# A GpSimd drain inside the last layer, one load of sums for four heads, and another order of the first loads

## The chip, the cores and the metric

The kernel runs on 1 core of one Trainium2 chip. The core has five engines with a queue of instructions each: TensorE (PE; its weight loads are listed as PEld), VectorE (DVE), ScalarE (ACT), GpSimd (POOL) and SyncE (SP). SP, ACT and POOL issue DMAs, which all run on the core's 16 DMA engines. The metric is device time in microseconds (us) of one execution, the median of several runs.

## The reference

Four graph layers run one after another on a matrix `x` of 4096 nodes by 256 features, with one random 0/1 adjacency of 4096 x 4096 (density 0.0078). Behind each layer stands `x = layernorm(x + layer(x))`. Cut to what matters here:

```python
# layer 0: attention over ALL pairs; pairs without an edge count with logit 0
node_feats = (x @ W.T + b).reshape(N, 8, 32)
logits = leaky_relu(parent[:, None, :] + child[None, :, :], 0.2)
logits = where(adj != 0, logits, 0.0)
out = einsum('ijh,jhc->ihc', softmax(logits, axis=1), node_feats)
# layer 1: (diagonal(adj) + adj) @ (x @ weight) + bias
# layer 2: two steps of a top-p attention (0.9) and of a diffusion, then layer norm
# layer 3: relu(concat([x, adj @ x / max(deg, 1)]) @ W + b)
```

## The kernel before

**Layer 0** is done in two passes. `sums0` walks over all row blocks with float32 matmuls (L601). Per row and head it makes the part of the softmax sums that belongs to the pairs without an edge above a threshold, and stores it in DRAM as `zd` (block, row, head, 33 values: 32 features and the sum of weights). It also stores the factors `gmd` in bfloat16, the adjacency as bytes in `nad`, and the parents' logits in `lpd`.

The second pass, the *heads* (578 to 1288 us), loops over `half` (2 halves of four heads), `it` (4 tiles of 1024 rows) and `hh` (4 heads): 32 heads in time. For each head and each of 8 groups of 4 neighbour blocks a mask `gt` is made. A comparison of the parents' logits `lpb` with the children's `nlc` gives `sg`, on ACT (L276, five groups of eight) or on DVE (L270, three), and DVE ANDs it with the adjacency bytes `na` (L278, L272). PE multiplies the mask with the factors `gm` (L331, 32 matmuls for a group, 256 for a head). Then DVE sums up the head: L337 (reduce), L341, L344, L345 (adds `z`, the tile loaded from `zd`), L347 and L348 (divide, into `y`).

The loads of this pass: `na` (L301) and `gm` (L303, L306) on SP; `lpb` (`row_logits`, L236) and `z` (L316) on POOL, both with two buffers, one load for each head; `X` and the first half's `y0` on SP (L308, L310). In the very first head the masks of groups 0 and 1 (`gt0`), their factors (`gm0`) and the first `lpb` (`first`) are there already; this is what `begun = 2` says, and why the loop over the loads starts with group 2 there. `mask` buffers: four `gt`, three `sg`. In the second half POOL also adds up `X` (L362, L363) and does layer norms (L88, L89, L96).

`add_w1` loads the weights of layer 1 and of the attention of layer 2: `load_w` and `load_row` on ACT (L115, L121), the rest on POOL (L783, L784). It stands in the code at the last tile of the second half, but the heads are not in a `manual_schedule`: the framework orders each engine's instructions there, and these loads depend on nothing that comes late, so the profile shows them issued at 579 to 600 us.

**Layer 3** (`layer3`, from 3723 us) is not in a `manual_schedule` either. For each row block `b` from 6 to 31 PE does 32 matmuls (L1973). `ready(b + 2)` has the pieces of the adjacency cast from bytes two blocks ahead, half on DVE (L1940) and half on ACT (L1942), into 8 buffers. `close(b, ps)` loads `x` (L1979, queued on ACT), scales on ACT (L1981), adds on DVE (L1982 to L1986), normalises (L85 and L86 on DVE, `ln_var` L88 and `ln_rstd` L89 on POOL, `y` L96 on DVE) and stores on ACT's queue (L1989). The first six passes of the loop also close one of the blocks 0 to 5, whose products layer 2 made. POOL issues no DMA in this layer.

At the end of the tile context (L2051) the framework itself puts a drain and a meeting of all engines.

Of the kernel before, what the change touches and what calls it, by code (L numbers as in the profile page):

```python
# [9 lines left out]
F32 = mybir.dt.float32  # L10
# [13 lines left out]
P = 128  # L24
# [26 lines left out]
def row_broadcast(v, n):  # L51

    return bass.AP(tensor=v.tensor, offset=v.offset, ap=[[0, P], [1, n]])


class Net:
# [159 lines left out]
    def layer0(self):  # L216
        nc, tc, NB, D, N = self.nc, self.tc, self.NB, self.D, self.N
        H, C = 8, 32
        C1 = C + 1
        IT = min(1024, N)  # L220
        Q = IT // P
        keep = self.ctx.enter_context(tc.tile_pool(name="l0k", bufs=1, space=DRAM))
        self.fits = keep.tile([1, 1], I32, name="fits")
        with ExitStack() as ctx:
            pool = ctx.enter_context(tc.tile_pool(name="l0", bufs=1))
# [6 lines left out]
            fac = pool.tile([P, 4, NB, H], F32, name="fac")  # L232
            lpd = dram.tile([H, N], F32, name="lpd")

            def row_logits(t, h, it):
                nc.gpsimd.dma_start(t, bass.AP(tensor=lpd.tensor, offset=lpd.offset + h * N + it * IT, ap=[[0, P], [1, IT]]))  # L236
                return t

            first = pool.tile([P, IT], F32, name="lpb0")
# [5 lines left out]
            zd = dram.tile([NB, P, H, C1], F32, name="zd")  # L245
# [42 lines left out]
            work = ctx.enter_context(tc.tile_pool(name="l0w", bufs=2))  # L288
# [2 lines left out]
            gm = gp.tile([P, NB, H // 2, 6 * C1], BF16, name="gm")  # L291
            na = gp.tile([P, NB, IT], U8, name="na")

            later = []
            per_head = Q // 2 // (H // 2)
            for half in range(2):
                for it in range(N // IT):
                    i0 = it * Q
                    begun = 2 if it == half == 0 else 0
                    for g in [*range(begun, NB // K), *range(begun)]:  # L300
                        nc.sync.dma_start(na[:, g * K:(g + 1) * K], nad[it, :, g * K:(g + 1) * K, :])  # L301
                        if it == 0:
                            nc.sync.dma_start(gm[:, g * K:(g + 1) * K, 0], gmd[half, :, g * K:(g + 1) * K, 0])  # L303
                    for hh in range(1, H // 2 if it == 0 else 0):
                        for g in range(0, NB // K, 2):
                            nc.sync.dma_start(gm[:, g * K:(g + 2) * K, hh], gmd[half, :, g * K:(g + 2) * K, hh])  # L306
                    if half:
                        nc.sync.dma_start(X[:, i0:i0 + Q, :], xr[:, i0:i0 + Q, :])  # L308
                        y0 = work.tile([P, Q, D // 2], F32, name="y0", bufs=1)
                        nc.sync.dma_start(y0, yd[i0:i0 + Q].rearrange("b p d -> p b d"))  # L310
                    y = work.tile([P, Q, H // 2, C], F32, name="y")
                    for hh in range(H // 2):
                        h = half * (H // 2) + hh
                        lpb = row_logits(work.tile([P, IT], F32, name="lpb"), h, it) if h or it else first
                        z = work.tile([P, Q, C1], F32, name="z")
                        nc.gpsimd.dma_start(z, zd[i0:i0 + Q, :, h].rearrange("b p c -> p b c"))  # L316
                        acc = psum.tile([P, Q, 256], F32, name="acc")
                        for g in range(NB // K):

                            head0 = g < 2 and half == it == hh == 0  # L320
                            if head0:
                                gt = gt0[:, g * K:(g + 1) * K, :]
                            else:
                                gt = work.tile([P, K, IT], FP8, name="gt", bufs=4)
                                sg = work.tile([P, K, IT], FP8, name="sg", bufs=3)
                                mask(gt, sg, na[:, g * K:(g + 1) * K, :], lpb, g, h)
                            for k in range(K):
                                jc = g * K + k
                                for q in range(Q):

                                    nc.tensor.matmul(acc[:, q, :6 * C1], gt[:, k, q * P:(q + 1) * P],  # L331
                                                     gm0[:, jc, :] if head0 else gm[:, jc, hh, :],
                                                     start=(jc == 0 and q % 2 == 0),
                                                     stop=(jc == NB - 1 and q % 2 == 1))

                        red = work.tile([P, Q, 2 * C1], F32, name="red")
                        nc.vector.tensor_reduce(red, acc[:, :, :6 * C1].rearrange("p q (s c) -> p q c s", s=3),  # L337
                                                AX.X, ALU.add)

                        red = red.rearrange("p q (s c) -> p q s c", s=2)  # L340
                        nc.vector.tensor_mul(red, red, fac[:, 0:2, i0:i0 + Q, h].rearrange("p s q -> p q s").unsqueeze(3)  # L341
                                             .to_broadcast([P, Q, 2, C1]))
                        t1 = red[:, :, 0, :]
                        nc.vector.tensor_add(t1, t1, red[:, :, 1, :])  # L344
                        nc.vector.tensor_add(t1, t1, z)  # L345
                        r = work.tile([P, Q], F32, name="r")
                        nc.vector.reciprocal(r, t1[:, :, C])  # L347
                        nc.vector.tensor_mul(y[:, :, hh, :], t1[:, :, :C], r.unsqueeze(2).to_broadcast([P, Q, C]))  # L348
                        for xs in later[:per_head]:
                            self.layernorm(work, xs, xs, nc.gpsimd, bufs=6)  # L350
                        del later[:per_head]
                    y = y.rearrange("p q h c -> p q (h c)")
                    if not half:
                        nc.gpsimd.dma_start(yd[i0:i0 + Q].rearrange("b p d -> p b d"), y)
                        continue

                    if i0 + Q == NB:
                        self.add_w1()
                    engine = nc.vector if i0 + Q == NB else nc.gpsimd
                    for q in range(0, Q, 2):  # L360
                        xs = X[:, i0 + q:i0 + q + 2, :]
                        nc.gpsimd.tensor_add(xs[:, :, :D // 2], xs[:, :, :D // 2], y0[:, q:q + 2])  # L362
                        engine.tensor_add(xs[:, :, D // 2:], xs[:, :, D // 2:], y[:, q:q + 2])  # L363
                        later.append(xs)
            self.later = later
            acc = psum.tile([P, Q, 256], F32, name="acc").rearrange("p q c -> p (q c)")
            for c in range(2):
                half = acc[:, c * 512:(c + 1) * 512]
# [408 lines left out]

    def add_w1(self):
        nc, pool = self.nc, self.pool1
        self.weight1, self.bias1 = self.load_w(pool, self.w1, "w1"), self.load_row(pool, self.b1, "bias1")  # L780
        aw1, aw3, aw2, _ = self.attention_parts()
        for t, w in ((aw1, self.aw1t), (aw3, self.aw3t)):
            nc.gpsimd.dma_start(t, w.rearrange("(c p) m -> p c m", p=P))  # L783
        nc.gpsimd.dma_start(aw2, self.aw2t)  # L784

    def attention_parts(self):

# [1157 lines left out]
    def layer3(self):  # L1945
        nc, tc, NB, D = self.nc, self.tc, self.NB, self.D
        G = 8
        with self.ctx3 as ctx:
            pool = ctx.enter_context(tc.tile_pool(name="l3", bufs=1, side="right"))
            work = ctx.enter_context(tc.tile_pool(name="l3s", bufs=2, side="right"))  # L1950
# [26 lines left out]
            def close(b, ps):  # L1977
                x = work.tile([P, 2, D], F32, name="x", bufs=3)
                nc.scalar.dma_start(x, self.xo[b])  # L1979
                low = work.tile([P, D], F32, name="low")  # L1980
                nc.scalar.mul(low, ps[:, D:], rdeg[:, b:b + 1])  # L1981
                nc.vector.tensor_add(x[:, 1], x[:, 1], bias)  # L1982
                h = work.tile([P, 1, D], F32, name="h")
                nc.vector.tensor_add(x[:, 1], x[:, 1], low)
                nc.vector.scalar_tensor_tensor(h[:, 0], ps[:, :D], rdeg[:, b:b + 1], x[:, 1], op0=ALU.mult, op1=ALU.add)  # L1985
                nc.vector.scalar_tensor_tensor(h[:, 0], h[:, 0], 0.0, x[:, 0], op0=ALU.max, op1=ALU.add)  # L1986
                y = work.tile([P, 1, D], F32, name="y")
                self.layernorm(work, y, h)
                nc.scalar.dma_start(out[:, b, :], y[:, 0])  # L1989
# [3 lines left out]
            for b in range(6, NB):  # L1993
                ps = products(b)
                if b + 2 < NB:
                    ready(b + 2)
                if rest:
                    k = rest.pop(0)
                    close(k, self.early3[k])
                close(b, ps)  # L2000


@with_exitstack
# [51 lines left out]
```

## Time and profile before

| what | value |
|---|---|
| median of 3 runs (lowest, highest) | 3931.0 us (3929.32, 3931.58) |
| the profiled execution: its time, its span | 3932.46 us, 3930.8 us |
| busy PE, PEld | 3872.5 us (99%), 3360.1 us (85%) |
| busy DVE, ACT, POOL | 2995.1, 2742.3, 1162.8 us |
| mean granted TensorE clock | 0.995 |
| layer 0's heads, 578 to 1288 us: busy PE, DVE, ACT, POOL | 702.9, 685.4, 664.1, 178.3 us |
| layer 3 and the end, 3720 to 3931 us: busy PE, DVE, ACT, POOL | 197.3, 112.9, 66.1, 26.3 us |

The span runs from the first to the last instruction of the program; the execution's own time is 1.66 us longer. A row of a timeline gives start, duration, engine, line, operation, written and read tiles, and in brackets how long the engine had been idle and who ended that. An engine name with a q (POOLq) is its sequencer: drains, semaphores and branches, which the page does not count as busy. A row of a window gives its length, then busy time (and instructions) of PE, PEld, DVE, ACT and POOL, the granted clock, the share of the DMA engines and GB/s.

### The profile page before, as it was taken

What the parts mean: (1) busy time and instruction counts of PE and PEld (TensorE: products, weight loads), DVE (VectorE), ACT (ScalarE), POOL (GpSimd) and SP (SyncE); (2) the same over time, 40 slices, a digit from 0 to 9 for tenths busy, and PEclk for the clock granted to TensorE, in tenths of its full rate; (3) what the DMA queues carried; (4) which work ended last, traced back from release to release, by engine and by line L of the source; (5) the groups of instructions that cost most, each with busy time, mean ns of one, the idle gap of its engine ahead of it and who ended that gap; (6) DMA issues with size and microseconds to landing.
All of it is one profiled execution on the core that took longest, in us unless ns stands there. A gap on an engine that the chain in (4) does not pass through costs nothing. (4 is left out here: it accounts for less than half of the span.)

```text
span 3930.8 us, 68793 instructions
## 1 busy us (share of the span) xinstructions
PE 3872.5 (99%) x25081; PEld 3360.1 (85%) x25081; DVE 2995.1 (76%) x6637; ACT 2742.3 (70%) x5121; POOL 1162.8 (30%) x1402
## 2 busy tenths in 40 slices
PE   8999999999999999999999999999999999999998
PEld 7999989999999887578888888876888888888786
DVE  6444449999999544768787878848999999999464
ACT  4443449999999322568888888836888888888232
POOL 1222220111444222411111111114566555555211
PEclk9999999999999999999999999999999999999999
DMA  4666657334221696533333232463333333336541
GB/s 119 201 206 205 219 187 214 93 108 129 73 82 60 247 384 266 151 114 109 105 101 100 95 103 93 138 220 109 109 112 114 112 115 101 107 108 205 208 149 45
DMA packets 319870, 561.58 MB, mean 143 GB/s; under 512 B 73063, under 2 KB 140151, under 8 KB 315415
## 3 DMA queue, kind: packets, MB, share of 16 engines
q1 hardware_dynamic: 244832, 401.18, 31.4%
q0 software_dynamic: 32224, 98.75, 7.8%
q10 hardware_dynamic: 42454, 57.04, 4.2%
q8 instruction: 203, 3.33, 0.3%
q14 instruction: 157, 1.28, 0.1%
HBM read 386.71 MB, written 170.13 MB: 142 GB/s over the span
## 5 line engine op out<-in xcount | busy, mean ns | idle before, releaser
L1414 PE MATMUL ps_a<-X,aT 128*128 128x256 f32 x4096 | 969.1, 379 | 1.6 <-ACT h L1558 1.1
L1414 PEld LDWEIGHTS ps_a<-X,aT 128*128 128x128 f32 x4096 | 773.2, 190 | 127.4 <-issue 3.3
L331 PE MATMUL acc<-gm,gt 128*128 128x198 bf16 x8192 | 702.9, 248 | 12.4 <-DVEq L375 5.4
L331 PEld LDWEIGHTS <-gt 128*128 128x128 fp8e4 x8192 | 700.8, 97 | 14.5 <-issue 9.7
L276 ACT ACTIVATE sg<-lpb,nlc 128x1024 fp8e4<-128x1024 f32 x632 | 664.1, 1135 | 45.4 <-DVE gt L278 32.5
L180 PE MATMUL ps_r<-XD,adj_piece 128*128 128x512 f32 x1888 | 528.4, 414 | 0.0
L601 PE MATMUL pz<-src,ar 128*128 128x264 f32 x4096 | 500.6, 285 | 0.4 <-DVE big L399 0.4
L601 PEld LDWEIGHTS pz<-src,ar 128*128 128x128 f32 x4096 | 500.4, 189 | 0.5 <-issue 0.5
L1139 ACT ACTIVATE ja<-e,nc 128x2048 uint8<-128x2048 f32 x240 | 480.9, 2004 | 2.0
L1407 ACT COPY aT<-ps_tp 128x512 f32<-128x512 f32 x512 | 295.9, 578 | 207.6 <-PE ps_tp L1405 201.6
L180 PEld LDWEIGHTS ps_r<-XD,adj_piece 128*128 128x128 f32 x1888 | 333.0, 189 | 68.8 <-issue 12.9
L1204 DVE MAX8 cand<-v 128x8 f32<-128x256 f32 x1024 | 347.1, 411 | 4.4
L1254 DVE SCALAR_TENSOR_TENSOR e<-e,edge 128x512 f32<-128x512 f32 x512 | 346.8, 749 | 2.1
L561 ACT ACTIVATE nb<-ar 128x512 uint8<-128x512 f32 x256 | 147.6, 623 | 280.0 <-DVE ar L558 164.6
L1405 PE MATMUL ps_tp<-ident,e 128*128 128x128 f32 x2048 | 307.3, 273 | 2.4 <-DVEq L1270 1.7
L1200 DVE SCALAR_TENSOR_TENSOR v<-e,hi 128x2048 f32<-128x2048 f32 x128 | 301.4, 2355 | 2.4
L1405 PEld LDWEIGHTS ps_tp<-ident,e 128*128 128x128 f32 x2048 | 255.9, 141 | 54.1 <-issue 2.6
L558 DVE CAST ar<-a 128x1024 fp32r<-128x1024 f32 x128 | 88.9, 694 | 267.3 <-PE pz L601 267.2
L270 DVE TENSOR_SCALAR sg<-lpb,nlc 128x1024 fp8e4<-128x1024 f32 x384 | 285.3, 778 | 6.7 <-SPq L375 4.6
L1048 ACT ACTIVATE e<-ps_logit 128x1024 f32<-128x1024 f32 x256 | 259.9, 1025 | 27.1 <-PE ps_logit L1046 26.8
L1046 PE MATMUL ps_logit<-kT,q 128*128 128x512 f32 x1024 | 273.9, 409 | 1.5 <-ACT e L1048 0.9
L854 PE MATMUL ps_adj<-XD,adj_piece 128*128 128x512 f32 x1024 | 239.8, 394 | 0.0
(408 smaller groups left out, 5587.4 us busy)
## 6 DMA issues: line engine op xcount, KB each, us to landing
adj_piece<-adjs SPq DMA_DIRECT2D x504, 256.0 KB, 2.8
a<-in_adjt_dram SPq DMA_DIRECT2D x256, 256.0 KB, 3.0
adjs<-adj_piece SPq DMA_DIRECT2D x96, 512.0 KB, 3.3
na<-nad SPq DMA_DIRECT2D x64, 512.0 KB, 5.4
lpb<-lpd POOLq DMA_DIRECT2D x32, 512.0 KB, 4.4
nad<-nb POOLq DMA_DIRECT2D x128, 128.0 KB, 2.7
na<-nad ACTq DMA_DIRECT2D x16, 1024.0 KB, 8.8
gmd<-gb POOLq DMA_DIRECT2D x64, 198.0 KB, 2.7
```

Source lines behind the costliest of these rows:

```text
L180: nc.tensor.matmul(ps, a[:, k, :], rhs(jc).rearrange("p s d -> p (s d)"), start=(jc == 0), stop=(jc == self.NB - 1))
L270: nc.vector.tensor_scalar(sg[:, k, :], lpb, nlc[:, 4 * g + k, h:h + 1], 2.0 ** -5, op0=ALU.is_ge, op1=ALU.mult, saturate=False)
L276: nc.scalar.activation(sg[:, k, :], lpb, AF.Sign, scale=-1.0, bias=nlc[:, 4 * g + k, h:h + 1], saturate=False)
L331: nc.tensor.matmul(acc[:, q, :6 * C1], gt[:, k, q * P:(q + 1) * P], gm0[:, jc, :] if head0 else gm[:, jc, hh, :], start=(jc == 0 and q % 2 ...
L601: nc.tensor.matmul(pz[q][:, t, :W], ar[:, q, k, :], src[:, jc, t, s], start=(jc == 0 and s == 0), stop=(jc == NB - 1 and s == 1))
L1139: nc.scalar.activation(ja, e[:, s * HALF:(s + 1) * HALF], f, bias=nc1, accum_out=fs[:, i + s:i + s + 1])
L1200: nc.vector.scalar_tensor_tensor(v, ec, hi, ec, op0=ALU.is_lt, op1=ALU.mult, accum_out=sb[:, s:s + 1])
L1204: nc.vector.max(cand[:, 8 * j:8 * j + 8], v[:, k * 256:(k + 1) * 256])
L1254: nc.vector.scalar_tensor_tensor(ec, ec, edge[:, j:j + 1], ec, op0=ALU.is_ge, op1=ALU.mult)
L1405: nc.tensor.transpose(pt[:, k * P:(k + 1) * P], e[:, jc * P:(jc + 1) * P], self.ident)
L1407: nc.scalar.copy(aT, pt)
L1414: nc.tensor.matmul(pa[:, :D], aT[:, k * P:(k + 1) * P], X[:, jc, :], start=(jc == 0), stop=(jc == NB - 1))
```

## The change

Three things. In layer 3, behind the closing of row block 20, stands one `nc.gpsimd.drain()`. In layer 0's heads, `z` holds the sums of four heads and is loaded once for each half and tile, into one buffer; the add L345 reads its own head's part. And the queues of first loads differ: in the first tile, `z` and the second head's `lpb` (`second`) are issued by SP behind the `na` and `gm` of group 4; in the other tiles `z` is issued by POOL; the weights that `add_w1` loads are all issued by SP.

```diff
--- before.py
+++ after.py
@@ -232,8 +232,8 @@
             fac = pool.tile([P, 4, NB, H], F32, name="fac")
             lpd = dram.tile([H, N], F32, name="lpd")
 
-            def row_logits(t, h, it):
-                nc.gpsimd.dma_start(t, bass.AP(tensor=lpd.tensor, offset=lpd.offset + h * N + it * IT, ap=[[0, P], [1, IT]]))
+            def row_logits(t, h, it, queue=nc.gpsimd):
+                queue.dma_start(t, bass.AP(tensor=lpd.tensor, offset=lpd.offset + h * N + it * IT, ap=[[0, P], [1, IT]]))
                 return t
 
             first = pool.tile([P, IT], F32, name="lpb0")
@@ -291,6 +291,11 @@
             gm = gp.tile([P, NB, H // 2, 6 * C1], BF16, name="gm")
             na = gp.tile([P, NB, IT], U8, name="na")
 
+            def products_of(i0, half, queue):
+                z = work.tile([P, Q, H // 2, C1], F32, name="z", bufs=1)
+                queue.dma_start(z, zd[i0:i0 + Q, :, half * H // 2:(half + 1) * H // 2].rearrange("b p h c -> p b h c"))
+                return z
+
             later = []
             per_head = Q // 2 // (H // 2)
             for half in range(2):
@@ -301,6 +306,11 @@
                         nc.sync.dma_start(na[:, g * K:(g + 1) * K], nad[it, :, g * K:(g + 1) * K, :])
                         if it == 0:
                             nc.sync.dma_start(gm[:, g * K:(g + 1) * K, 0], gmd[half, :, g * K:(g + 1) * K, 0])
+                        if begun and g == 4:
+                            z = products_of(i0, half, nc.sync)
+                            second = row_logits(work.tile([P, IT], F32, name="lpb"), 1, 0, nc.sync)
+                    if not begun:
+                        z = products_of(i0, half, nc.gpsimd)
                     for hh in range(1, H // 2 if it == 0 else 0):
                         for g in range(0, NB // K, 2):
                             nc.sync.dma_start(gm[:, g * K:(g + 2) * K, hh], gmd[half, :, g * K:(g + 2) * K, hh])
@@ -311,9 +321,8 @@
                     y = work.tile([P, Q, H // 2, C], F32, name="y")
                     for hh in range(H // 2):
                         h = half * (H // 2) + hh
-                        lpb = row_logits(work.tile([P, IT], F32, name="lpb"), h, it) if h or it else first
-                        z = work.tile([P, Q, C1], F32, name="z")
-                        nc.gpsimd.dma_start(z, zd[i0:i0 + Q, :, h].rearrange("b p c -> p b c"))
+                        lpb = (first, second)[h] if it == 0 and h < 2 else \
+                            row_logits(work.tile([P, IT], F32, name="lpb"), h, it)
                         acc = psum.tile([P, Q, 256], F32, name="acc")
                         for g in range(NB // K):
 
@@ -342,7 +351,7 @@
                                              .to_broadcast([P, Q, 2, C1]))
                         t1 = red[:, :, 0, :]
                         nc.vector.tensor_add(t1, t1, red[:, :, 1, :])
-                        nc.vector.tensor_add(t1, t1, z)
+                        nc.vector.tensor_add(t1, t1, z[:, :, hh, :])
                         r = work.tile([P, Q], F32, name="r")
                         nc.vector.reciprocal(r, t1[:, :, C])
                         nc.vector.tensor_mul(y[:, :, hh, :], t1[:, :, :C], r.unsqueeze(2).to_broadcast([P, Q, C]))
@@ -777,11 +786,14 @@
 
     def add_w1(self):
         nc, pool = self.nc, self.pool1
-        self.weight1, self.bias1 = self.load_w(pool, self.w1, "w1"), self.load_row(pool, self.b1, "bias1")
+        self.weight1 = pool.tile([P, 2, self.D], F32, name="w1")
+        nc.sync.dma_start(self.weight1, self.w1.rearrange("(c p) m -> p c m", p=P))
+        self.bias1 = pool.tile([P, self.D], F32, name="bias1")
+        nc.sync.dma_start(self.bias1, row_broadcast(self.b1, self.D))
         aw1, aw3, aw2, _ = self.attention_parts()
         for t, w in ((aw1, self.aw1t), (aw3, self.aw3t)):
-            nc.gpsimd.dma_start(t, w.rearrange("(c p) m -> p c m", p=P))
-        nc.gpsimd.dma_start(aw2, self.aw2t)
+            nc.sync.dma_start(t, w.rearrange("(c p) m -> p c m", p=P))
+        nc.sync.dma_start(aw2, self.aw2t)
 
     def attention_parts(self):
 
@@ -1998,6 +2010,8 @@
                     k = rest.pop(0)
                     close(k, self.early3[k])
                 close(b, ps)
+                if b == 20:
+                    nc.gpsimd.drain()
 
 
 @with_exitstack
```

## Prediction

> **What bounds the kernel now.** I read the busy table first, then the chain of waits, then the rows around the places that the diff touches. TensorE (PE) is busy 3872.5 of 3930.8 us, so only PE's 58 us of idle time, or work behind its last matmul, can be won. The chain of waits ends with DVE's `y` at 3921.46 us, yet the span ends at 3930.8: the 9 us behind it are no arithmetic. Line L2051 (the end of the tile context) shows what they are, asked in two windows, 3919 to 3929.5 and from 3929.95:
>
> ```profile
> L2051 SPq DRAIN x2: 7/10/13, 3923.6 to 3923.7; - x2
> L2051 POOLq DRAIN x1: 9528/9528/9528, 3920.4 to 3920.4; - x1
> ...
> L2051 POOLq EVENT_SEMAPHORE x4: 17/17/17, 3930.0 to 3930.7; - x4
> L2051 POOLq DRAIN x2: 44/78/113, 3930.1 to 3930.5; - x2
> ```
>
> SP has seen the last outputs land and is drained at 3923.67; ACT and DVE are earlier. POOL's last operation ends at 3921.01, but its drain lasts from 3920.40 to 3929.93, and only then do the engines meet (3929.97 on). So 3929.93 - 3923.67 = 6.26 us of the span wait for that drain alone.
>
> The second place is the start of layer 0's heads. The timeline of PE, and line L331 (the heads' matmul) in the windows 589.4 to 595.3 and 660 to 680:
>
> ```profile
> 578.14 7.36 PE L331 MATMUL acc<-gm,gt 128*128 128x198 bf16 x64 [5.38 <-DVEq L375]
> 589.51 10.66 PE L331 MATMUL acc<-gm,gt 128*128 128x198 bf16 x90 [4.01 <-DMA gm<-gmd]
> ...
> L331 PE MATMUL acc<-gm,gt x36: 325/370/373, 589.5 to 595.2; 128*128 128x198 bf16 x36
> ...
> L331 PE MATMUL acc<-gm,gt x238: 248/248/249, 659.8 to 679.9; 128*128 128x198 bf16 x119
> ```
>
> The first two groups (64 matmuls, masks made beforehand) run out at 585.5; the third waits 4.01 us for its factors `gm`. The matmuls behind the gap start every 163 ns (36 in 5.7 us), later ones every 85 ns (238 in 20.1 us): the gap costs 4.2 us from start to start and 36 x 80 ns = 2.9 us of halved clock. What fills the DMA engines then, in the timelines of POOL and SP and the windows:
>
> ```profile
> 579.74 1.41 POOL L316 DMA_DIRECT2D z<-zd  x1 [9.48 <-SPq L375]
> 581.13 0.62 POOL L236 DMA_DIRECT2D lpb<-lpd  x1
> 581.75 1.02 POOL L316 DMA_DIRECT2D z<-zd  x1
> 582.76 0.55 POOL L236 DMA_DIRECT2D lpb<-lpd  x1
> ...
> 579.94 1.26 SPq L303 DMA_DIRECT2D gm<-gmd  x1
> 584.23 3.57 SPq L301 DMA_DIRECT2D na<-nad  x1
> ...
> 586.00:590.00 4.00, 0.49 (x4) 0.44 (x4) 0.72 (x2) 2.03 (x2) 0.00 (x0) 0.83 1.04 320
> 590.00:594.00 4.00, 4.00 (x26) 3.65 (x25) 2.45 (x3) 1.19 (x2) 0.00 (x0) 0.50 1.11 341
> ```
>
> The `gm` that PE lacks was issued at 579.94. Share of the DMA engines (second last column) is full, at 320 to 341 GB/s. Summed from the packet records of the trace, 582 to 591 us: POOL's queue moved 1.45 MB, SP's 1.26 MB. POOL's part is `z`, two `lpb` and layer 1's weights, none of it needed before 590.
>
> **The drain.** It adds one instruction to POOL and removes what it does from the end. What the long drain does in its 8.92 us beyond POOL's last operation, no row says; the nearest rows bound it. POOL's last DMA (of 515) landed at 3667.6, 250 us earlier, so it waits for no transfer. The two drains right behind it take 113 and 44 ns, and the one at 0.4 us, before any POOL DMA, 168 ns. So the cost goes with what POOL has issued since the last drain, and a drain behind all of POOL's DMAs should leave nothing for the end: layer 3 issues none on POOL. Bounds: 6.26 us gained (the end drain falls to 0.05 to 0.2 us, and SP at 3923.67 is last), or nothing (the cost stays at the end). I take 6.26, by the 44 to 168 ns rows.
>
> What does the new drain cost in its place? Its operands tie it to nothing, so there are two places. Behind block 20 POOL is free from 3840.25; 8.92 us later is 3849.2. Queued behind it are `ln_var` and `ln_rstd` of block 21, which ran at 3846.84: 2.3 us late. DVE's `y`, the store behind it on ACT and the next casts wait for them: the cast at 3848.26, third piece of block 24, moves to 3850.6. PE takes 7.467 us per block and reaches that piece at 3861.5. Covered, with 10 us to spare. If it goes earlier, to the start of layer 3, POOL is idle from 3707.9 to 3734.9, and 9 us fit there too. Were the cover gone (between two early closes, where casts are about 4 us ahead of PE), it would cost 5 us and a cold restart of 2.9. I take 0.
>
> The Trainium skill speaks against this part: its page "VectorE: DVE Perf Modes", section "The DRAIN you can't avoid", says that the drains around a kernel are about 12 ns, constant, on all engines. By that the sum of this part would be 0. The trace agrees for SP, DVE and ACT in the second meeting and disagrees for POOL: 9528 ns.
>
> **The first loads.** Edits: one `z` of four heads (528 KB) for four of 132 KB; `z` and the second `lpb` go from POOL to SP, behind the third `na`/`gm` pair; the weights of layer 1 (0.26 MB on ACT, 0.14 MB on POOL, a bias of 0.13 MB) go to SP's queue, where they stand behind the loads of `X` near 630 us. There SP has nothing to issue from 630.8 to 648.7, so that move costs nothing. POOL is left with one early `lpb` (0.5 MB).
>
> I lay SP's queue out at 340 KB/us from 581 us. `lpb` from POOL takes most of the first 2 us, so SP has moved 0.38 MB by 583.5 and the first `na`+`gm` (0.73 MB) by 584.5; landing about 1 us behind (as `na` 3: bytes through at 590.4, landed at 591.5) gives 585.5 to 586.5. PE then waits 0 to 1 us instead of 4.01 and keeps its clock: 7.1 us less 1. What is late next: the inserted `z` and `lpb` (1.04 MB, 3.1 us) push the fifth pair's `na`: through at 593.8, mask 1.22 us (an AND on DVE) done at 596, wanted at 594.5: 1.3 us of stall. All bytes ahead of the second head's `gm` come to 7.4 MB now and 7.3 then, so its first piece lands near 605.5, wanted at 604: 1.5 us more. 7.1 - 1 - 1.3 - 1.5 = 3.3; I take 3.2 us. Bounds: 0 (the same bytes through the same engines, the wait only moves) and 7.1 (no wait at all). Masks on ACT (4.2 us for each of 5 groups in a head of 21.76) stay ahead of PE in this layout.
>
> Here too the skill has a rule against it: "DMA: Bandwidth & Descriptors", section "Issuing engines are not separate DMA queues", says that DMAs of all engines run on the same 16 and interleave. By it only the deferred 0.4 MB counts, which at 340 KB/us would be 1.2 us.
>
> **The later tiles.** `z` has one buffer now, so each of seven reloads waits for the last head of the tile before (DVE's L345), and is needed one head (21.76 us) later; it lands in 3.2 to 5.5 us. Hidden, if nothing urgent stands behind it on POOL. Twenty-four fewer DMAs of 0.9 us on POOL free nothing: POOL waits for DVE there. Cost 0.
>
> **Sum.** The profiled execution took 3932.46 us (span 3930.8), 1.5 above the median of 3931.0. 3932.5 - 6.3 - 3.2 = 3923.0 profiled, 3921.5 for the median.
>
> **The rivals.** *The wait only moves* (15%): the drain gives 6.3, the first loads under 1.6, because the fifth `na` and the second head's `gm` come no earlier: 3923.1 to 3924.7. For it: the DMA engines are full until 637 us. Against: 1.45 MB beside `gm` becomes 0.5.
>
> *The whole gap goes* (10%): loads give 5.5 to 7.1: 3917.6 to 3919.2.
>
> *The drain does not do what it says* (10%): POOL's 9 us is a price of the end, whatever was drained before, or the drain is sent where it costs PE what it saves: 3931 - 3.2 = 3927.8. For it: one execution of it only. Against: 44, 113 and 168 ns.
>
> *Slower* (6%): the single `z` stands at the head of POOL's queue at each tile boundary, with the next two `lpb` behind it. Then the masks of the next head start only when the last head is summed (8.9 us behind its last matmul), `z` and `lpb` issued and landed (0.9 + 4.4), and a mask made (4.2 + 1.2): 20 us of idle PE and 2.9 of cold clock, 7 times: 3931 + 160 - 9 = 4082. It decides as soon as `z` is queued ahead of one of those `lpb`. Against it, POOL's timeline, where the store of `y` (L354), which stands in the code ahead of `lpb` and `z` of the next two heads, is issued behind them, because it was not ready:
>
> ```profile
> 660.88 1.23 POOL L316 DMA_DIRECT2D z<-zd  x1 [15.67 <-DVE gt L272]
> 665.64 0.56 POOL L236 DMA_DIRECT2D lpb<-lpd  x1 [3.54 <-ACT sg L276]
> 681.14 0.89 POOL L316 DMA_DIRECT2D z<-zd  x1 [14.94 <-DVE red L345]
> 683.35 0.89 POOL L354 DMA_DIRECT2D yd<-y  x1 [1.31 <-DVE y L348]
> ```
>
> **The numbers.** The forecast (drain 6.3, loads 1.6 to 5.5) has 59%. A measurement here can tell about 0.2%, 7.9 us, from no change: faster by that needs 1.6 us of the loads besides the drain. So faster 0.59 + 0.10 = 0.69, taken as 0.67 for causes unseen; same 0.15 + 0.10 = 0.25; slower 0.06 + 0.02 = 0.08. Range: from 3917.6 (whole gap) to 3927.8 (drain without effect).
>
> **What would show it.** Right: POOL's drain at the end under 0.3 us, SP's at the end of the chain, a POOL drain near 9 us in layer 3 with PE dense; PE's gap near 585 under 1.5 us with no 163 ns matmuls behind it, and the second head starting near 605.5 instead of 608.7. Wrong: a long drain at the end still; gaps of PE at 594 or 604 that eat the gain; a `z` ahead of `lpb` at a tile boundary with PE idle behind it.

## The result and the profile after

| | before | after |
|---|---|---|
| median of 20 runs (lowest, highest) | 3931.55 us (3928.59, 3936.65) | 3926.15 us (3924.16, 3931.70) |
| the profiled execution: its time, its span | 3932.46, 3930.8 us | 3926.08, 3924.4 us |
| POOL's drain at the end | 9528 ns | 5118 ns |
| PE's last matmul to the end of the span | 13.48 us | 9.09 us |
| first matmul of the heads to the second head | 30.54 us | 28.03 us |

The ratio of the times is 0.9987 [0.9981, 0.9993]: 5.4 us less, 0.14%. The changed kernel is faster, but by less than the 0.2% that the prediction called no change.

First the new drain. These are the instructions of line L2014, and those of L2065 (end of the tile context) between 3918 and 3923.7 us; the columns are count, shortest/median/longest in ns, first and last start in us.

```profile
L2014 POOLq DRAIN  x1: 281/281/281, 0.8 to 0.8; - x1
...
L2065 SPq DRAIN  x2: 7/10/13, 3921.3 to 3921.4; - x2
...
L2065 POOLq DRAIN  x1: 5118/5118/5118, 3918.4 to 3918.4; - x1
```

The drain that the code has behind row block 20 ran at 0.8 us, before POOL had issued any DMA. Still the drain at the end is 4.4 us shorter. SP is done at 3921.37, POOL at 3923.53: 2.2 us of the span still wait for POOL alone, against 6.26 before.

Then the start of the heads: PE's timeline from 576 to 612 us (L340 is the heads' matmul; in brackets the idle time and who ended it).

```profile
577.98 7.00 PE L340 MATMUL acc<-gm,gt 128*128 128x198 bf16 x64 [5.28 <-DVEq L384]
586.18 8.48 PE L340 MATMUL acc<-gm,gt 128*128 128x198 bf16 x96 [1.20 <-DMA gm<-gmd]
596.11 2.89 PE L340 MATMUL acc<-gm,gt 128*128 128x198 bf16 x32 [1.45 <-DVE gt L272]
599.32 5.61 PE L340 MATMUL acc<-gm,gt 128*128 128x198 bf16 x64 [0.32 <-DVE gt L278]
606.01 6.23 PE L340 MATMUL acc<-gm,gt 128*128 128x198 bf16 x71 [1.07 <-DMA gm<-gmd]
```

And the windows (length, busy time and instructions of PE, PEld, DVE, ACT, POOL, granted clock, DMA share, GB/s):

```profile
586.00:590.00 4.00, 3.81 (x44) 3.60 (x44) 2.39 (x4) 2.25 (x3) 0.00 (x0) 1.00 1.10 336
590.00:594.00 4.00, 4.00 (x50) 4.00 (x49) 3.75 (x5) 3.30 (x4) 0.00 (x0) 1.00 1.10 374
```

The wait for `gm` is 1.20 instead of 4.01 us, and the granted clock stays at 1.00 where it was 0.83 and 0.50: 94 matmuls run in these 8 us instead of 30. In exchange there are stalls at 596, 599 and 606 us that before did not have.

At a tile boundary `z` is no obstacle. PE is dense from 611.82 to 1137 us, past six of the seven reloads, and its two later stalls of 0.75 and 1.69 us, behind a mask each, stood in the kernel before too (1.04 and 1.72 us). POOL's timeline at the first boundary shows the reload and the `lpb` behind it:

```profile
679.77 0.91 POOL L296 DMA_DIRECT2D z<-zd  x1 [14.89 <-DVE red L354]
681.98 1.51 POOL L363 DMA_DIRECT2D yd<-y  x1 [1.30 <-DVE y L357]
685.35 0.56 POOL L236 DMA_DIRECT2D lpb<-lpd  x1 [1.86 <-ACT sg L276]
```

### The profile page after: what moved, and what is told of

Read it like the earlier page. It is cut to its first block, busy times and chain, and to the rows that moved or that the text cites. A ratio compares the mean times of both kernels' runs of the same rounds, so it can differ in the third digit from the quotient of the medians.

```text
span 3924.4 us, 68724 instructions
## 1 busy us (share of the span) xinstructions
PE 3870.3 (99%) x25081; PEld 3356.7 (86%) x25081; DVE 2994.2 (76%) x6637; ACT 2742.8 (70%) x5121; POOL 1123.1 (29%) x1373
## 5 line engine op out<-in xcount | busy, mean ns | idle before, releaser
L340 PE MATMUL acc<-gm,gt 128*128 128x198 bf16 x8192 | 700.0, 248 | 11.8 <-DVEq L384 5.3
L340 PEld LDWEIGHTS <-gt 128*128 128x128 fp8e4 x8192 | 698.1, 97 | 13.7 <-issue 8.0
```

## The experiments

### One part at a time

**The drain alone**, as the change writes it:

```diff
@@ layer3, before @@
                 close(b, ps)
+                if b == 20:
+                    nc.gpsimd.drain()
```

> The kernel before with the drain alone, written as in the change. Theory A (it has no operands, so the framework issues it at the very start, before POOL has issued any DMA, and it does nothing): a POOL drain of 0.2 to 0.3 us at about 0.8 us, the end's drain again 9.5 us long, ratio to before 0.9995 to 1.0005. Theory B (the early drain sets something that makes the end's drain short): the end's drain near 5.1 us, 4.4 us faster, ratio 0.9989.

```profile
L2002 POOLq DRAIN  x1: 279/279/279, 0.8 to 0.8; - x1
...
L2053 POOLq DRAIN  x3: 40/113/9527, 3921.3 to 3931.4; - x3
```

The ratio to before is 1.0000 [0.9991, 1.0009], and the end drain keeps its 9.53 us. The drain as written does nothing. It reads and writes no tile and layer 3 stands in no `manual_schedule`, so nothing held it behind block 20, and the framework put it at the front of POOL's queue.

**The loads alone**, the changed kernel without its drain:

```diff
@@ layer3, after @@
-                if b == 20:
-                    nc.gpsimd.drain()
```

> The changed kernel without the drain. Theory A: the end's drain is 5.1 us as in the changed kernel, because POOL issues fewer DMAs before it; second head at 606.0 us; ratio to before 0.9985 to 0.9990, as the changed kernel. Theory B: the end's drain is back at 9.5 us and 4.4 us are lost: ratio about 0.9997.

```profile
L2063 POOLq DRAIN  x3: 40/113/5118, 3918.3 to 3924.0; - x3
```

3927.92 us, 0.9991 [0.9982, 1.0000]. So the edits of the loads shorten the end drain to the 5118 ns of the changed kernel, without any drain.

**The drain where it was meant to be**, kept in program order ("pinned" from here on), in the changed kernel and in the kernel before:

```diff
-                    nc.gpsimd.drain()
+                    tc.keep_in_program_order(nc.gpsimd.drain())
```

> The changed kernel with the drain held behind block 20's closing by an ordering edge. Theory A (the cost goes with what POOL issued since the last drain): a POOL drain of about 4.5 us behind 3838 us in layer 3, PE dense there, the end's drain under 0.3 us, and the end set by SP at its own drain: 2.2 us less than the changed kernel, ratio to before about 0.9981. Rival C (the cost belongs to the end, whatever was drained before): the end's drain stays 5.1 us, nothing is won.

> The kernel before with the drain held behind block 20's closing. This is the term of 6.3 us in the prediction by itself. Theory A: a POOL drain of 8.9 us in layer 3 from about 3840 us, the layer norm of block 21 about 2.3 us late, PE without a gap, the end's drain under 0.3 us, 6.2 us less than before: ratio 0.9984. Rival C: the end's drain stays 9.5 us, ratio 1.0000. Rival D (the drain delays the casts): PE gaps in layer 3, ratio over 0.9990.

The two drains of POOL in the changed kernel (L2014, L2065), and the same in the kernel before (L2002, L2053):

```profile
L2014 POOLq DRAIN  x1: 5118/5118/5118, 3841.1 to 3841.1; - x1
...
L2065 POOLq DRAIN  x3: 34/113/676, 3921.8 to 3925.4; - x3
```

```profile
L2002 POOLq DRAIN  x1: 9530/9530/9530, 3842.4 to 3842.4; - x1
...
L2053 POOLq DRAIN  x3: 34/112/676, 3922.6 to 3926.4; - x3
```

The price moves as it stands, to the nanosecond, from the end into layer 3, and 0.68 us are left at the end. Under 0.3 was expected, but 0.61 of them lie beside POOL's last operation, so 0.07 stand behind it. The tail behind PE's last matmul is 6.89 us in the changed kernel and 7.18 in the other: 13.48 - 7.18 = 6.30 us won. The times: 3925.31 us, 0.9981 [0.9972, 0.9990], and 3925.93 us, 0.9982 [0.9973, 0.9991]. What the drain held up, in POOL's timeline of the kernel before with the pinned drain:

```profile
3842.44 0.57 POOL L89 TENSOR_TENSOR ln_rstd<-ln_var,power 128x1 f32<-128x1 f32 x1
3852.35 0.22 POOL L88 TENSOR_SCALAR ln_var<-ln_mv 128x1 f32<-128x1 f32 x1 [9.34 <-issue]
```

`ln_var` of the next block had its input at 3848.99 and ran 3.4 us late; PE had no gap over 50 ns in this layer.

### What the price of the drain hangs on

The changed kernel issues 29 DMAs fewer on POOL (486 instead of 515), and 4410 ns / 29 = 152 ns for each was the first theory (A). Two of the change's edits were made alone in the kernel before. Of the kernels of this part only the last was timed; the others ran once, for their profiles, and their times are not compared. **Wide `z`**, from POOL, 24 DMAs fewer:

```diff
-                        z = work.tile([P, Q, C1], F32, name="z")
-                        nc.gpsimd.dma_start(z, zd[i0:i0 + Q, :, h].rearrange("b p c -> p b c"))
+                    z = products_of(i0, half, nc.gpsimd)   # once for each half and tile
```

> The kernel before, with one edit of the change alone: z is loaded for four heads at once, all from GpSimd's queue. That takes 24 DMAs from GpSimd (32 loads of z become 8). Theory A (the drain at the end costs about 152 ns for each DMA that GpSimd issued since its last drain, as 9528 ns against 5118 ns at 29 fewer DMAs say): end drain 9.53 - 24 x 0.152 = 5.9 us, from PE's last matmul to the end of the span 9.8 instead of 13.5 us. Rival B (the price hangs on which loads went, those of the weights of layer 1, not on how many): end drain stays at 9.5 us. The wait of PE for gm near 589 us stays near 4 us, since as many bytes of z stand ahead as before, or more.

**The weights on SP**, 3 DMAs fewer:

```diff
-            nc.gpsimd.dma_start(t, w.rearrange("(c p) m -> p c m", p=P))
-        nc.gpsimd.dma_start(aw2, self.aw2t)
+            nc.sync.dma_start(t, w.rearrange("(c p) m -> p c m", p=P))
+        nc.sync.dma_start(aw2, self.aw2t)
```

(and the other two loads of `add_w1` likewise)

> The kernel before, with another edit of the change alone: the loads of layer 1's weights go to SP's queue, which takes 3 DMAs from GpSimd. Theory A (152 ns for each DMA): end drain 9.53 - 0.46 = 9.07 us. Rival B (the loads of the weights are what the drain pays for): end drain near 5.1 us or below. The wait of PE near 589 us gets shorter by what 0.4 MB at 340 KB/us cost, 1.2 us: about 2.8 instead of 4.0 us.

The end drains, the first and the second kernel:

```profile
L2055 POOLq DRAIN  x3: 40/113/6672, 3925.5 to 3932.7; - x3
```

```profile
L2054 POOLq DRAIN  x3: 44/113/7732, 3922.7 to 3931.0; - x3
```

Both theories missed: 24 DMAs fewer save 2.86 us, 119 ns each, and 3 fewer save 1.80 us, 599 ns each. PE's longest wait for `gm` was 5.73 us with the wide `z` on POOL and 3.36 us with the weights on SP, where about 2.8 was expected. But eight profiles of kernels whose first loads are those of before have a longest wait of 2.90 to 5.37 us there, so neither value shows what its edit does to that wait. The third kernel put **drains among the sums of layer 0**. These stand in a `manual_schedule`, so the drains stay where the code has them:

```diff
@@ sums0, behind the matmuls of step b, before @@
+                    if b in (0, 4, 12, 30):
+                        nc.gpsimd.drain()
```

> The kernel before, with four drains of GpSimd added while the sums of layer 0 are made, at points between which it issues some 12, 12, 24 and 60 DMAs. It measures the price of a drain by itself. Theory A (about 152 ns for each DMA since the last drain): about 1.8, 1.8, 3.6 and 9 us, if every DMA counts, and the end drain is smaller than 9.53 us only if the DMAs before the sums' end counted in it. Rival C (only some last part of the DMAs counts, because what it pays for can be full or is cleared by something else): the four drains are not in the ratio 1 : 1 : 2 : 5, and the end drain stays at 9.53 us.

```profile
L605 POOLq DRAIN  x4: 3776/4150/4259, 105.3 to 570.0; - x4
...
L2053 POOLq DRAIN  x3: 56/113/2983, 3920.3 to 3924.1; - x3
```

After 13, 24, 48 and 107 DMAs the four drains take 3.78, 4.26, 4.12 and 4.18 us: no count of DMAs is in that. But the end drain falls to 2.98 us, so the effect of these drains is kept over the 3.3 ms behind the last of them.

These values fit a sum that fills and starts again (theory D). Each DMA on POOL adds its rows, as its record gives them (dst_num_elem: 128 for an `lpb`, 1024 for a `z`, of either width); when the next one would take the sum over some 6700 (6656 to 6783 all give the same), it restarts at zero; a drain costs 0.94 us + 1.43 ns for each row then in the sum, and empties it. Limit and prices, three numbers, were fitted to the first five lines of this table; the last four were forecast with them:

| kernel | rows in the sum | theory D | measured |
|---|---|---|---|
| before | 6016 | 9.54 us | 9.53 us |
| after (and pinned) | 2944 | 5.15 | 5.12 |
| wide `z` | 3968 | 6.61 | 6.67 |
| weights on SP | 4736 | 7.71 | 7.73 |
| drains in the sums, at the end | 1408 | 2.95 | 2.98 |
| four stores more | 6528 | 10.27 | 9.85 |
| eight stores more | 384 | 1.49 | 1.53 |
| drain in layer 1 | 2176 | 4.05 | 3.61 |
| the same, at the end | 3712 | 6.25 | 6.67 |

The version of the next section fits too. It issues one DMA fewer on POOL than the changed kernel, at a place ahead of the last restart; by D its sum is 2944 again, and its pinned drain takes the 5.12 us of the changed kernel:

```profile
L2017 POOLq DRAIN  x1: 5117/5117/5117, 3835.0 to 3835.0; - x1
```

**Stores on POOL's queue** put it to the test: by it, more DMAs must at some point make the drain shorter.

```diff
@@ close, layer 3, before; 12 for four stores, 16 for eight @@
-                nc.scalar.dma_start(out[:, b, :], y[:, 0])
+                (nc.gpsimd if 8 <= b < 16 else nc.scalar).dma_start(out[:, b, :], y[:, 0])
```

> The kernel before, with four of layer 3's output stores (blocks 8 to 11, 128 rows of 1 KB each) issued by GpSimd instead of ACT: four more DMAs on GpSimd. Theory D (a store that fills and empties: each DMA adds its rows (the product of dst_num_elem in its record); when the next would take the sum over some 6700, it starts again from zero; the drain costs 0.94 us and 1.43 ns for each row of the sum; fitted to the end drains of before, after, e3 to e8): the sum rises from 6016 to 6528 and the end drain from 9.53 to 10.3 us. Theory A (152 ns for each DMA): 10.1 us. Rival E (the price is set by the start of layer 0's heads alone, where many loads are under way at once): 9.53 us still.

> The same with eight stores (blocks 8 to 15) issued by GpSimd. Theory D: the sixth of them (the 6784th row) does not fit any more, the sum starts again and ends at 384, and the end drain falls to 1.5 us, although GpSimd has issued eight DMAs more than in the kernel before; the span ends some 6 us earlier behind PE's last matmul (7.2 instead of 13.5 us). Theory A: 10.7 us. Rival E: 9.53 us.

With four, and with eight:

```profile
L2051 POOLq DRAIN  x3: 40/113/9853, 3918.0 to 3928.5; - x3
```

```profile
L2051 POOLq DRAIN  x3: 40/113/1527, 3919.5 to 3923.3; - x3
```

Four DMAs more and the drain grows by 0.33 us; four further ones and it falls by 8.3. No price for each DMA and no cause at the start of the heads does that. The tail behind PE is 7.19 us, as with the pinned drain, though no drain was added. **A drain in layer 1**, where POOL has issued 263 DMAs and the last of them has landed 52 us earlier:

```diff
@@ layer1, before `pd` @@
+            tc.keep_in_program_order(nc.gpsimd.drain())
```

> The kernel before, with one GpSimd drain kept in program order in layer 1, before its first row block (near 1320 us; 263 of 515 DMAs are issued by then, the last landed some 60 us earlier). Theory D: 4.05 us there (sum 2176) and 6.25 us at the end (sum 3712). Rival E (the price is set by the start of the heads, and only a drain takes it away): 7 us or more there, 3 us or less at the end. Theory A: 263 x 0.152 = 40 us there, or, if only loads of z and weights count, 5 us there and 5 at the end.

The drain in layer 1, POOL's operations beside it, and the drains at the end:

```profile
L838 POOLq DRAIN  x1: 3612/3612/3612, 1312.5 to 1312.5; - x1
...
1312.56 2.80 POOL L96 TENSOR_SCALAR X<-X,ln_mv,ln_rstd 128x256 f32<-128x256 f32 x2
...
L2052 POOLq DRAIN  x3: 56/112/6665, 3926.8 to 3934.1; - x3
```

3.61 and 6.67 us. Rival E forecast 7 or more there and 3 or less at the end, theory A 40 (or 5) us there; neither came. D is 0.4 us off at both, and at the four stores. The row of layer 1 is no clean price, though. POOL's own operations (L96, the row above) run until 1315.36, 2.86 us into that drain, and only 0.75 us of it lie beyond them. The end drains have some 0.6 us of POOL's last operation beside them, so D's price beyond POOL's work would be 0.33 us + 1.43 ns for each row, 3.44 us here. Either the drain worked beside these operations, or D is 2.7 us too high; the runs don't tell which. So the four and the eight stores show that something fills and starts over; that it counts rows, and at this price, is a fit to the drains in layer 3 and at the end. What D leaves unexplained are the four drains among the sums, for which it gives 8.3, 5.1, 9.2 and 4.4 us. They began while POOL's own stores were under way (the last landed 1.9 to 2.9 us later) and ended 1.2 to 2.3 us behind that landing; why they were so short stays open.

**The eight stores, timed:**

> The kernel of e10_eight_stores, now timed: no drain is added to it, only eight output stores moved to GpSimd's queue. Theory D: it ends as early as e4_before_pinned, whose drain was paid inside layer 3 (ratio 0.9982 to the kernel before): 6.3 us less than before, a ratio of 0.9984. Rival: the stores wait on GpSimd for DVE's results and hold up its small steps, so that PE loses in layer 3 what the end gains: ratio 0.999 or more. End drain 1.5 us again, as it hangs on the rows issued and not on time.

```profile
L2051 POOLq DRAIN  x3: 40/113/1523, 3921.3 to 3925.1; - x3
```

3926.45 us, 0.9987 [0.9978, 0.9996]. The interval holds theory D's 0.9984 and the rival's 0.999. The tail is 7.19 us again, and PE has no gap over 50 ns in layer 3 in this profile, so the rival's mechanism is not there (the profile of the untimed run has one gap there, of 0.20 us).

### The first loads, moved further

The changed kernel with the pinned drain, and later places for three loads:

```diff
-                        if begun and g == 4:
-                            z = products_of(i0, half, nc.sync)
+                        if begun and g == 5:
                             second = row_logits(work.tile([P, IT], F32, name="lpb"), 1, 0, nc.sync)
...
                             nc.sync.dma_start(gm[:, g * K:(g + 2) * K, hh], gmd[half, :, g * K:(g + 2) * K, hh])
+                            if begun and hh == 1 and g == 2:
+                                z = products_of(i0, half, nc.sync)
+                            if begun and hh == 1 and g == 6:
+                                third = row_logits(work.tile([P, IT], F32, name="lpb"), 2, 0, nc.sync)
```

(`lpb` of head 2 is then `third`)

> The changed kernel with the drain held in program order behind block 20 (as in e3_after_pinned), and with the first loads moved further: the second lpb stands behind the sixth pair of masks, z behind the second piece of the second head's gm, and the third lpb comes from SP behind that gm instead of early from GpSimd. Theory A (the stalls that are left at 586, 596 and 606 us are bytes that stand ahead of what PE wants): the stalls of 1.45 and 1.07 us fall under 0.5 each and the second head starts near 603.5 us instead of 606.0; 2 to 3 us less than e3_after_pinned, a ratio to the kernel before of about 0.9974. Rival (the loads are bound by their own bytes, or another load is late next): the second head starts at 605.5 or later, and the ratio is that of e3_after_pinned, 0.9981.

```profile
577.86 23.34 PE L343 MATMUL acc<-gm,gt 128*128 128x198 bf16 x256 [5.30 <-DVEq L387]
601.86 4.35 PE L343 MATMUL acc<-gm,gt 128*128 128x198 bf16 x49 [0.66 <-DMA gm<-gmd]
```

The first head runs through without a stall, and the second starts 24.0 us behind the first, at 601.86 us where 603.5 was forecast. The stall of 1.45 us is gone, that of 1.07 fell to 0.66, not under 0.5 as expected. 3922.06 us, 0.9975 [0.9965, 0.9984]: this is the lowest ratio of all versions, 10.5 us under the kernel before, though its interval overlaps that of the changed kernel with the pinned drain (0.9981 [0.9972, 0.9990]). The profile is as theory A of this expectation has it: the stalls were bytes ahead of what PE wanted. It is one profile, but its 24.0 us lie 3 us below the lowest of the three with the change's first loads (26.96 to 28.56, below).

## Why the prediction was half right

Forecast: 9.5 us less, 3921.5 us. Measured: 5.4 us less, 3926.15 us. The time is within the range and below before, but the likeliest case did not come, and 4.4 of the 5.4 us came in another way than the one given. That the time fell within the range is luck: the shorter end drain, for which the prediction had no reason, brought it there. Without these 4.4 us the changed kernel would be near 3930.5, above the range (3917.6 to 3927.8).

**Where the drain goes: wrong.** The prediction said that "its operands tie it to nothing", and from that took two places, block 20 or the start of layer 3. The step that failed is the bound: what is tied to nothing can go to the very front, and it did (0.8 us). The drain's own effect was 0, as the rival "the drain does not do what it says" had it. The Trainium skill's rule (page "VectorE: DVE Perf Modes", section "The DRAIN you can't avoid"), by which this part came to 0, has the result of this part right and its reason wrong: POOL's drain is not about 12 ns, it lasts from 0.03 to 9.85 us in these runs.

**What the drain is worth where it was meant: right.** 6.26 us forecast, 6.30 measured with it pinned. So was its cover: 8.92 us beyond POOL's last operation, now inside layer 3 (3843.01 to 3851.93), `ln_var` 3.4 us late in place of 2.3, PE unhurt.

**That fewer DMAs on POOL "free nothing": wrong.** This stood in the part on the later tiles, where it is right; at the end, with the other edits of the loads, they freed 4.4 us. The prediction had said that the cost goes with what POOL issued since the last drain, and then did not apply this to its own count of DMAs removed. No row of before shows anything that starts over, so 4.4 could not have been worked out; a range from 0 to 6.3 could.

**The first loads: right in place, too large in size.** The stalls came where they were laid out: 1.20 us at 586 (0 to 1 forecast), 1.45 and 0.32 for the fifth and sixth groups (1.3), 1.07 for the second head (1.5), and no halved clock behind the first of them. What was mis-sized is the base, 4.2 us of gap and 2.9 of halved clock. The profile of before needs 30.54 us from the first head to the second, and the changed kernel 28.03. But seven more profiles are of kernels with the first loads of before, and they need 28.87 to 31.58 us, a mean of 29.71 over all eight; three profiles are of kernels with those of the change and need 26.96 to 28.56, a mean of 27.85. That is 1.9 us, not 3.2. In five of the eight the third group is there in time or 0.42 us late, and the long gap stands ahead of the fourth and is shorter, as with the drain alone:

```profile
579.00 10.41 PE L331 MATMUL acc<-gm,gt 128*128 128x198 bf16 x96 [5.32 <-DVEq L375]
592.82 19.34 PE L331 MATMUL acc<-gm,gt 128*128 128x198 bf16 x206 [3.41 <-DMA gm<-gmd]
```

Behind the gap 36 matmuls are slow in the profile of before (29 in that with the drain in layer 1), but 20 or 21 in the other six: with the drain alone the granted clock is 0.50 for 3.41 us, in before for 6.83. The gap and the slow matmuls with the drain alone come to 3.6 + 1.6 = 5.2 us in place of 7.1. The new stalls were also counted by PE's idle time, where the old gap was counted from start to start, which adds 0.16 us for each of four stalls (a matmul lasts 248 ns and the next starts after 85). The times show less still: pinned drain with and without the new loads, 3925.31 against 3925.93 us, 0.6 less, and the loads alone against the drain alone (which did nothing), 3927.92 against 3932.46, 4.5 less, of which 4.4 are the end drain and 0.1 is left; the interval of each is some 3.5 us to either side. By the Trainium skill's "DMA: Bandwidth & Descriptors", section "Issuing engines are not separate DMA queues", an estimate for these loads is 1.2 us, for the 0.4 MB that go later. The runs give 0.1 to 1.9 us and can't tell this from 0 or from 1.9; with the weights alone on SP the second head came after 28.84 us, 0.9 less than the mean, but only 0.03 below the lowest of the eight.

**The later tiles: right.** No wait for `z`, and a `z` was never ahead of an `lpb` that PE then lacked. The slow rival (4082 us) did not show.

**The sum.** 6.3 became 4.4 and 3.2 became 1.0 (5.4 - 4.4, by the medians). The chance of "same" was 0.25; it rested on a lost drain or a wait that only moves, and what came is a little of both.

## What to carry to other kernels

An instruction without operands need not be where the code has it: outside a `manual_schedule` the drain of this change ran at 0.8 us until it was kept in program order. Look for its start time before anything is said of its effect. A long drain of POOL at the end of a kernel is a price that can be paid where POOL is idle (here 6.3 us for one line), or made small by what POOL's DMAs carry, and then an edit that adds or removes one can change it: three fewer took 1.8 us off it, four more added 0.3, eight more took 8.0 off. Where a start-up differs by 2.7 us between eight profiles of one order of loads, a single profile can't size a gain of 3 us: lay out the order by bytes and needs, and take the size from several profiles.

## What was not expected of the hardware

POOL's drain at the end takes 9.53 us though POOL's last DMA landed 250 us earlier, 9.85 us with four stores more, the last of them landed 134 us earlier, and 1.53 us when a further four DMAs are issued ahead of it. A sum of rows that restarts at some 6700 describes the drains in layer 3 and at the end within 0.42 us, and does not describe those among the sums of layer 0. That it stands for rings of descriptors that POOL's software writes for its DMAs (so the Trainium skill, page "DMA: Bandwidth & Descriptors", section "SWDGE vs HWDGE vs iDMA") is only argued: no run here shows a ring.
